# Dense q and k for layer 1, scattered into per-head strips by on-chip transfers

## Chip, core and metric

The kernel runs on one core of a Trainium2 chip. The core has a matrix engine (PE in the profile, with its weight loads as PEld), a vector engine (DVE), a scalar engine (ACT), GpSimd (POOL) and the sync engine (SP), which here only issues transfers. The metric is the device time of one execution in microseconds (us). The kernel before takes 1684.3 us, the median of three runs (1683.4 to 1684.37).

## What is computed

Sixteen sequences of 512 tokens with 128 channels pass through two layers. Layer 0 is linear attention followed by a mixture of eight experts with two chosen per token, plus a shared expert. Layer 1 is attention with sixteen heads of eight channels, in chunks of 64 queries, and a channel mix after it. The change touches only how the q and k of layer 1 are made. Cut to that:

```python
# layer 1 attention, for each chunk of 64 queries [s:e]
scores = einsum('bhtd,bhsd->bhts', q[:, :, s:e], k[:, :, :e]) / 8 ** 0.5   # 16 heads, d = 8
probs  = softmax(scores)                     # then a gate on the row sums
out    = einsum('bhts,bhsd->bhtd', probs, v[:, :, :e])
```

All data are float32.

## The kernel before, in words

The whole program is one stream of Python calls that are first recorded and then put in order. Every call on an engine becomes an `Op` with a cost, and `Program.run` (L330) is a list scheduler: for each engine it keeps the operations whose inputs are ready by its own reckoning, and emits the one recorded first (L407, with a preference for DVE operations that empty PSUM). The emitted order is fixed per engine, so on the chip each engine goes through its list in that order and stands still when the next one's input isn't there. The reckoning of a transfer is at L274: 80 ns on SP, and a size at 250 bytes per ns plus 2000 ns until it has landed (L379 to L385). PE's costs are at L261 to L271, with a charge for every change of the tile's shape (`TURN`, L220).

Four chains of work are recorded in turns: dispatch of tokens to experts, the expert tiles (`slot_tiles`, L1122), layer 0 (`first_layer`, L1499), and layer 1 (`layer1`, L1554). In layer 1 each sequence b has a `head` (L1510), which adds the experts' results, makes the layer norm `xp`, the channel mix, the values and the operands of the first half of the heads, and a `body` (L1529), which runs the two halves u = 0 and 1 of eight heads. `weighted(b, u)` (L1349) computes the scores again in transposed form (`st`), their exponentials (`ex`, ACT) and the output (`o`). Beside it runs the next thing: `operands(b, 1)` during `weighted(b, 0)`, with two of its steps for each of five units, and `head(b + 1)` during `weighted(b, 1)`, with three.

`operands` (L1294) is what is changed. There are 32 sets (b, u). A set holds eight heads as four strips of 32 partitions, two heads to a strip. In `qa` the rows 0 to 15 of a strip are the q of its two heads; the others carry a mask and, later, minus the row maximum. In `ka` there are two copies, one for each head of the pair; each copy has the other head's rows at zero, and rows that hold constant ones. To get this layout straight from the matmul, the weights `wqk1` are padded with zero columns (L584 to L588): 4 blocks of 128 columns for q and k of both halves. A set then needs these instructions:

```python
ps = big(f"qk1_{b}_{u}")
for i in range(2):                                   # q, k: 128x128 by 128x512
    M.matmul(ps[:, i, :], wqk1[:, 2 * i + u, :, :]..., xT, start=True, stop=True)
V.tensor_tensor(qa, ps[:, 0, :], c_("aug_q"), ALU.add)
for o in range(2):
    V.scalar_tensor_tensor(ka[:, o, :], ps[:, 1, :], c_("parity")[:, o : o + 1],
                           aug_k[:, o, :], ALU.mult, ALU.add)
```

After them come five units of score matmuls (`sc`) whose row maxima DVE takes (`maxima`), a transpose of the maxima (`mx`), and a subtraction in place, `qa -= pm` (L1345). `qa` and `ka` have two buffers each, so the `ka` of a set takes the place of the one two sets earlier, when the last `st` of that set is done. Before layer 1 starts, sequence 1 of layer 0 borrows the same buffers (`LENT`, L808).

SP issues every direct transfer: for each of 163 expert tiles a load of `wf` and one of `wp` (L1146, L1149; four buffers each), the token rows `xg`, the results `yg`, the passing of `xnT` and `x1` through DRAM, and the outputs.

Of the kernel before, what the change touches and what calls it, by code (L numbers as in the profile page):

```python
# [36 lines left out]
P = 128  # L37
# [15 lines left out]
def slot_count(gt):  # L53
# [29 lines left out]
_CONST = (  # L83
    ("ident", P), ("cos", NT * 4), ("sin", NT * 4), ("blocks", 8 * (PAIR + 2)), ("pick", 4),
    ("causal", P), ("rank", E), ("upper", P), ("ones", P), ("tile", SLOT_TILES),
    ("aug_q", T), ("aug_k", 2 * T), ("parity", 2),
)


# [68 lines left out]
class Base:  # L158


    def __init__(self, slots, make):
        self.slots, self.make, self.tile = slots, make, None
        self.writers, self.readers = [], []
        self.left, self.free_at, self.users = 0, 0.0, []

    def made(self):
# [58 lines left out]
class Program:  # L225
# [21 lines left out]
    def call(self, name, api, method, args, kw):  # L247
        views = [a for a in (*args, *kw.values()) if isinstance(a, View)]
        o = kw.get("out", args[0] if args else None)
        writes = [o.base] if isinstance(o, View) else []  # L250
        reads = [v.base for v in views if v is not o]
        n = math.prod(o.shape[1:]) if isinstance(o, View) else 0
        later = 0.0

        def made(a):
            return a.made() if isinstance(a, View) else a

        def emit():
            return getattr(api, method)(*map(made, args), **{k: made(a) for k, a in kw.items()})  # L259

        if name == "PE":  # L261
            later = 60.0
            form = (args[1].shape[0], o.shape[0])
            if method == "transpose":
                cost = 112.0
            elif args[1].shape[0] == 32:
                cost = max(0.425 * n, 56.0)
            elif o.shape[0] == 32:
                cost = max(0.425 * n, 56.0)
            else:  # L270
                cost = max(1.68 * n, 224.0)  # L271
        elif method == "dma_start":
            cost, later = 80.0, 512.0 * n
        else:  # L274
            form = method if (name, method) in COSTS else None
            if name == "DVE" and method in ("tensor_scalar", "tensor_scalar_min", "tensor_scalar_max"):
                form = "fast"
            if method in ("tensor_reduce", "bn_stats"):
                n = math.prod(args[1].shape[1:])
            least, each = COSTS[name, form]  # L280
            cost = least + each * n
            if kw.get("func", args[2] if len(args) > 2 else None) == AF.Sqrt:
                cost += 2600.0
        op = self.add(name, emit, reads, writes, cost, later)
        if name == "PE":
            (self.unit_of[0] if self.unit_of else op).form = form
        return op

    def add(self, name, emit, reads, writes, cost, later=0.0):
        if self.unit_of is not None:  # L290
            if self.unit_of == []:
                self.unit_of.append(self._new(name, None, 0.0, 0.0))
            op = self.unit_of[0]
            part = Op(name, emit, 0.0, 0.0, op.index)
            op.parts.append(part)
            op.cost += cost
        else:
            part = op = self._new(name, emit, cost, later)
        for base in reads:
            op.needs.update(base.writers)  # L300
        for base in writes:

            op.needs.update(o for o in base.writers if o.engine != "SP" or name != "SP")
            op.needs.update(base.readers)
        for base in reads:
            base.readers.append(op)
        for base in writes:
            if base.readers:
                base.writers, base.readers = [], []
            base.writers.append(op)  # L310
        op.needs.discard(op)
        op.bases.update(reads, writes)
        op.wrote.update(writes)
        return part
# [172 lines left out]
def two_layers(ctx: ExitStack, tc: tile.TileContext, x, small, const, w_fc, w_proj, out):  # L487
# [30 lines left out]
        i.behind = [(first, mybir.DependencyClass.NoSync)]  # L518


    const_sb = fixed.tile([P, _CONST_N], F32, tag="const", name="const_sb")
    small_sb = fixed.tile([P, _STAYS_N], F32, tag="small", name="small_sb")

    wfc_s = fixed.tile([P, FF], F32, tag="wfc_s", name="wfc_s")
# [10 lines left out]
        for n in ("xnT", "x1") for b in range(B) if n == "x1" or b > 1  # L535
    }
    x_in = {b: load_x(b, "x_in", 2) for b in range(2)}
    lo = _CONST_AT["aug_q"][0]
    SP.dma_start(const_sb[:, 0:lo], const[:, 0:lo])
    raw = {}  # L540
    for name in ("wqkv0", "wqk1"):
        program.lag = 400 if name == "wqk1" else 0
# [3 lines left out]
    for names in (_STAYS[:2], _STAYS[2:]):  # L546
# [1 line left out]
        (lo, _), (_, hi) = _SMALL_AT[names[0]], _SMALL_AT[names[-1]]  # L548
        (slo, _), (_, shi) = _STAYS_AT[names[0]], _STAYS_AT[names[-1]]
        SP.dma_start(small_sb[:, slo:shi], small[:, lo:hi])  # L550
    lo = _CONST_AT["aug_q"][0]
    SP.dma_start(const_sb[:, lo:], const[:, lo:])
    program.lag = 250
    SP.dma_start(wfc_s, w_fc[:, E, :])
    SP.dma_start(wpj_s, w_proj[:, E, :, :])
# [21 lines left out]
    rank = c_("rank").unsqueeze(1)  # L577
    cos = c_("cos").rearrange("p (t d) -> p t d", d=4)
    sin = c_("sin").rearrange("p (t d) -> p t d", d=4)
    aug_k = c_("aug_k").rearrange("p (o t) -> p o t", o=2)  # L580

    program.lag = 200

    wqk1 = fixed.tile([P, 4, 4, 32], F32, tag="wqk1", name="wqk1")  # L584
    G.memset(wqk1, 0.0)
    given1 = raw["wqk1"].rearrange("p (su j o e) -> p su j o e", su=4, j=4, o=2)
    for o in range(2):
        V.tensor_copy(wqk1[:, :, :, o * DH : (o + 1) * DH], given1[:, :, :, o, 0:DH])  # L588

    program.lag = 1000  # L590

# [699 lines left out]
            )  # L1291
        return vp

    def operands(xT, b, u):  # L1294

        ps = big(f"qk1_{b}_{u}")
        for i in range(2):
            M.matmul(
                ps[:, i, :], wqk1[:, 2 * i + u, :, :].rearrange("p j e -> p (j e)"), xT,
                start=True, stop=True,
            )
        qa = p2.tile([P, T], F32, tag="qa", name=f"qa_{b}_{u}")
        V.tensor_tensor(qa, ps[:, 0, :], c_("aug_q"), ALU.add)
        ka = p2.tile([P, 2, T], F32, tag="ka", name=f"ka_{b}_{u}")
        for o in range(2):  # L1310
            V.scalar_tensor_tensor(
                ka[:, o, :], ps[:, 1, :], c_("parity")[:, o : o + 1], aug_k[:, o, :],
                ALU.mult, ALU.add,
            )
        yield
        mx = maxima
        for i, unit in enumerate(QUERIES):
            scs = [big(f"sc1_{b}_{u}_{i}_{pr}") for pr in range(2)]
            with program.unit():
                for t, os_, at in unit:  # L1320
                    n, m = (t + 1) * P, len(os_)
                    for j in range(4):
                        r = 32 * j
                        M.matmul(
                            scs[j // 2][:, j % 2, at : at + m * n].rearrange(
                                "p (o k) -> p o k", o=m
                            ),
                            qa[r : r + 32, t * P : (t + 1) * P],
                            ka[r : r + 32, os_[0] : os_[0] + m, 0:n], start=True, stop=True,
                        )  # L1330
            for pr, sc in enumerate(scs):
                for t, os_, at in unit:
                    n, m = (t + 1) * P, len(os_)
                    V.tensor_reduce(
                        mx[:, t, 2 * pr : 2 * pr + 2, PAIR + os_[0] : PAIR + os_[0] + m],
                        sc[:, :, at : at + m * n].rearrange("p j (o k) -> p j o k", o=m), AX.X,
                        ALU.max,
                    )
            yield
        pm = one(f"mx1_{b}_{u}")  # L1340
        for t in range(NT):
            M.transpose(
                pm[:, t * P : (t + 1) * P], mx[:, t, :, :].rearrange("p j e -> p (j e)"), ident
            )
        V.tensor_tensor(qa, qa, pm, ALU.subtract)  # L1345
        yield
        return qa, ka

    def weighted(qm, ka, vp, b, u, ahead, n_ahead):  # L1349

# [159 lines left out]
    def head(b):  # L1510
# [8 lines left out]
        G.memset(xp[:, 0:1], 0.0)  # L1519
        yield from layernorm_T(x1, xp[:, 1 : T + 1], f"1_{b}", "xn1", 1)  # L1520
        yield
        base = yield from channel_mix(x1, xp, b)
        yield
        vp = values(xp[:, 1 : T + 1], b)
        yield
        qm, ka = yield from operands(xp[:, 1 : T + 1], b, 0)
        return xp, base, vp, qm, ka

    def body(b, state):  # L1529


        xp, base, vp, qm, ka = state
        o0, (qm, ka) = yield from weighted(
            qm, ka, vp, b, 0, operands(xp[:, 1 : T + 1], b, 1), 2
        )
# [64 lines left out]
def _constants():  # L1600
# [12 lines left out]
    c["blocks"] = (head == row[:, None, None]).astype(f).reshape(P, -1)  # L1613
    c["pick"] = ((i // DH) % 4 == np.arange(4)[:, None]).T.astype(f)
    aug_q, aug_k = np.zeros((4, 32, T), f), np.zeros((4, 32, 2, T), f)
    parity = np.zeros((4, 32, 2), f)
    for o in range(2):
        aug_k[:, PAIR + o, o] = 1.0
        parity[:, o * DH : (o + 1) * DH, o] = 1.0
    for t in range(NT):  # L1620
        aug_q[:, PAIR + 2 + t, t * P : t * P + P // 2] = HIDDEN
        aug_k[:, PAIR + 2 + t, :, t * P + P // 2 : (t + 1) * P] = 1.0
    c["aug_q"], c["aug_k"] = aug_q.reshape(P, T), aug_k.reshape(P, 2 * T)
    c["parity"] = parity.reshape(P, 2)
# [66 lines left out]
```

## Time and profile before

| | before |
|---|---|
| median of three runs | 1684.3 us |
| the profiled execution's own time | 1683.13 us |
| its span, first to last instruction | 1681.3 us |
| mean granted PE clock | 0.973 |
| PE busy | 1566.0 us (93%) |
| DVE busy | 1220.5 us (73%) |
| ACT busy | 763.4 us (45%) |
| POOL busy | 405.0 us (24%) |
| transfers of the SP queue | 148.67 MB, 29.7% of 16 engines |

The profile shows one execution. A group of instructions is named by the tile that it writes and those that it reads (`qk<-xp,wqk` writes the PSUM tile qk1 from xp and wqk1); L259 stands on almost every row, because one helper records every operation. One float32 matmul of the program stands as two PE records, so the 64 matmuls of `qk` are 128 records. PE records overlap, so the time that a group takes up on PE is read from the starts in the timeline, not from the sum of its durations.

### The profile page before, as it was taken

The numbers are of one execution on the slowest core, as the hardware profiler recorded it, in microseconds if no ns is written. First come the engines' busy times: TensorE is split into PE (matmuls) and PEld (weight loads), VectorE is DVE, ScalarE is ACT, GpSimd is POOL, SyncE is SP. The second block draws the span as 40 slices with busy tenths as digits, with TensorE's granted clock in tenths as the row PEclk, the third lists the DMA queues.
The fourth block names the chain that finished last, engine by engine and source line by source line (L and its number), as shares of the span: only waits on it lengthen the run. The fifth ranks groups of instructions, "written<-read, shape, count | busy, mean of one in ns | idle before, by whom it ended". The sixth has DMA issues, their size and how long they took to land.

```text
span 1681.3 us, 36447 instructions
## 1 busy us (share of the span) xinstructions
PE 1566.0 (93%) x14503; PEld 1027.3 (61%) x14503; DVE 1220.5 (73%) x2520; ACT 763.4 (45%) x1175; POOL 405.0 (24%) x389
## 2 busy tenths in 40 slices
PE   5898889999999999999999999999999999999996
PEld 3687766576756566665766656656665566555443
DVE  7876269767479875977678884968587867676773
ACT  3343334535445554445445553453545543534434
POOL 2404362162115211251014321140115010104000
PEclk8899999999999999999999999999999999999888
DMA  5377857143433532332332332313133223011000
GB/s 173 110 219 223 247 185 218 47 136 98 125 96 94 162 93 69 116 95 75 95 98 81 103 95 79 103 60 114 49 93 89 63 72 101 8 44 29 19 1 13
DMA packets 155129, 167.78 MB, mean 100 GB/s; under 512 B 13264, under 2 KB 100688, under 8 KB 154960
## 3 DMA queue, kind: packets, MB, share of 16 engines
q1 hardware_dynamic: 146768, 148.67, 29.7%
q0 software_dynamic: 8192, 16.79, 3.2%
q8 instruction: 114, 1.87, 0.4%
q14 instruction: 55, 0.45, 0.1%
HBM read 123.59 MB, written 41.81 MB: 98 GB/s over the span
## 4 chain that ended last, share of the span: by engine, by line
PE 55%; DVE 13%; ACT 3%; issue 1%; ACTq 0%; DVEq 0%
PE sc L259 11%; PE o L259 10%; PE st L259 8%; PE yg_ps L259 5%; DVE maxima L259 4%; PE hg_ps L259 4%; PE y L259 4%; PE qk L259 3%; PE h_ps L259 2%; ACT ex L259 1%; PE ho_a L259 1%; PE qkv L259 1%; PE oh_a L259 1%; PE mx L259 1%; PE cm_r L259 1%
## 5 line engine op out<-in xcount | busy, mean ns | idle before, releaser
L259 DVE TENSOR_REDUCE maxima<-sc 128x2 f32<-128x768 f32 (+2 forms) x448 | 385.4, 913 | 74.4 <-PE sc L259 71.4
L259 ACT ACTIVATE ex<-st 128x1024 f32<-128x1024 f32 x320 | 312.4, 1025 | 183.2 <-PE st L259 174.0
L259 PE MATMUL sc<-ka,qa 32*128 32x512 f32 (+2 forms) x1792 | 214.5, 518 | 7.5 <-DVE maxima L259 3.9
L259 PE MATMUL st<-qa,ka 32*128 32x384 f32 (+3 forms) x2048 | 209.3, 467 | 9.3 <-ACT ex L259 4.6
L259 DVE TENSOR_TENSOR am<-sc,const_sb 128x1024 f32<-128x1024 f32 x128 | 151.3, 1217 | 81.5 <-PE sc L259 76.6
L259 PE MATMUL yg_ps<-wp,hg 128*128 128x128 f32 x1304 | 182.1, 283 | 18.4 <-DVE hg L259 6.3
L259 PEld LDWEIGHTS yg_ps<-wp,hg 128*128 128x128 f32 x1304 | 160.0, 192 | 61.3 <-issue 32.1
L1091 POOL DMA_INDIRECT rows<-xn,pl_slot x128 | 131.4, 1026 | 224.0 <-DVE pl_slot L259 46.8
L259 PE MATMUL hg_ps<-xgT,wf 128*128 128x128 f32 x1304 | 176.1, 280 | 9.0 <-DMA wf<-in_w_fc 3.6
L1110 POOL DMA_INDIRECT back<-results,pl_slot x128 | 127.2, 994 | 220.2 <-PE st L259 45.6
L259 PEld LDWEIGHTS hg_ps<-xgT,wf 128*128 128x128 f32 x1304 | 158.7, 193 | 32.9 <-issue 13.4
L259 PE MATMUL o<-ex,vpad 128*32 128x512 f32 (+3 forms) x2048 | 175.7, 445 | 1.1 <-ACT oT_a L259 0.6
L259 PEld LDWEIGHTS st<-qa,ka 32*128 32x128 f32 x2048 | 103.6, 185 | 78.1 <-issue 27.0
L259 ACT ACTIVATE hg<-hg_ps 128x1024 f32<-128x1024 f32 x84 | 84.0, 1000 | 137.0 <-PE hg_ps L259 123.0
L259 PEld LDWEIGHTS sc<-ka,qa 32*128 32x128 f32 x1792 | 90.5, 188 | 69.0 <-issue 21.4
L259 POOL TENSOR_TENSOR hg<-hg 128x1024 f32<-128x1024 f32 x34 | 65.1, 1914 | 276.4 <-ACT hg L259 276.1
L259 PEld LDWEIGHTS o<-ex,vpad 128*32 128x32 f32 x2048 | 52.5, 109 | 88.0 <-issue 66.0
L259 DVE TENSOR_TENSOR hg<-hg 128x1024 f32<-128x1024 f32 (+1 forms) x50 | 58.4, 1168 | 59.3 <-ACT hg L259 45.7
L259 ACT COPY oTs<-o 128x256 f32<-128x256 f32 (+1 forms) x96 | 42.6, 444 | 125.4 <-PE o L259 113.6
L259 PE MATMUL sc<-q0m,k0T 32*128 32x256 f32 x1024 | 82.1, 412 | 3.3 <-ACT ex L259 1.4
L259 ACT COPY yg<-yg_ps 128x256 f32<-128x256 f32 x84 | 31.0, 369 | 112.5 <-PE yg_ps L259 77.0
L259 PE MATMUL o<-am,vpad 128*32 128x128 f32 x2048 | 77.0, 277 | 1.2 <-DVE am L259 0.9
(189 smaller groups left out, 2216.8 us busy)
## 6 DMA issues: line engine op xcount, KB each, us to landing
wf<-in_w_fc SPq DMA_DIRECT2D x163, 256.0 KB
wp<-in_w_proj SPq DMA_DIRECT2D x163, 256.0 KB
results<-yg SPq DMA_DIRECT2D x79, 128.0 KB
xg<-rows SPq DMA_DIRECT2D x37, 256.0 KB
rows<-zeros SPq DMA_DIRECT2D x2, 2496.0 KB
x_in<-in_x SPq DMA_DIRECT2D x16, 256.0 KB
x<-x SPq DMA_DIRECT2D x16, 256.0 KB
out<-rr SPq DMA_DIRECT2D x16, 256.0 KB
```

The source lines that it names most:

```text
L259: return getattr(api, method)(*map(made, args), **{k: made(a) for k, a in kw.items()})
L1091: i = nc.gpsimd.indirect_dma_start(out=rows.made()[:, :], out_offset=bass.IndirectOffsetOnAxis(ap=slot.made(), axis=0), in_=row.made(), in ...
L1110: "POOL", lambda: nc.gpsimd.indirect_dma_start(out=o.made(), out_offset=None, in_=results.made()[:, :], in_offset=bass.IndirectOffsetOnAxi ...
```

## The change

Per sequence, q and k of all sixteen heads are made by two matmuls from packed weights (`dense`), and two ACT copies put them into SBUF as `q1` and `k1`; this stands in `head`, after the layer norm and before the channel mix. `q1` uses the buffer of the layer norm's `xn`. The strips are now two lasting pairs of buffers, one for each half, filled once from the constants; in each set twelve transfers by SP overwrite only the rows of q and k: four of 16 rows and eight of 8 rows, each row 512 floats. The zero rows and the ones stay as they are. The subtraction of the maxima writes a tile of its own, `qm`. The three DVE operations of a set, the tile `parity`, the memset of the padded weights and the load of the masks at the start are gone. In the scheduler, writes that follow each other to one buffer all wait for the readers from before the first of them, and the landing time of a transfer now counts the partitions of its destination.

```diff
-            cost, later = 80.0, 512.0 * n
+            cost, later = 80.0, 4.0 * n * (o.shape[0] if isinstance(o, View) else P)
...
             op.needs.update(base.readers)
+            op.needs.update(base.before)
...
             if base.readers:
+                base.before = base.writers + base.readers
                 base.writers, base.readers = [], []
...
-    wqk1 = fixed.tile([P, 4, 4, 32], F32, tag="wqk1", name="wqk1")
-    G.memset(wqk1, 0.0)
...
+    wqk1 = fixed.tile([P, 2, P], F32, tag="wqk1", name="wqk1")
+    given1 = raw["wqk1"].rearrange("p (h e) -> p h e", e=32)
+    V.tensor_copy(
+        wqk1.rearrange("p s (h e) -> p (s h) e", e=DH), given1[:, :, 0:DH]
+    )
...
+    def make_strips():
+        for u in range(2):
+            qa = p2.tile([P, T], F32, tag="qa", name=f"qa_{u}")
+            ka = p2.tile([P, 2, T], F32, tag="ka", name=f"ka_{u}")
+            (lo, hi), (klo, khi) = _CONST_AT["aug_q"], _CONST_AT["aug_k"]
+            first = [
+                SP.dma_start(qa, const[:, lo:hi]),
+                SP.dma_start(ka.rearrange("p o t -> p (o t)"), const[:, klo:khi]),
+            ]
+            strips.append((qa, ka, first))
+
+    def dense(xT, b):
+
+        if not strips:
+            make_strips()
+        ps = big(f"qk1_{b}")
         for i in range(2):
...
+            M.matmul(ps[:, i, :], wqk1[:, i, :], xT, start=True, stop=True)
+        q = p2.tile([P, T], F32, tag="xn1", name=f"q1_{b}", bufs=1)
+        k = p2.tile([P, T], F32, tag="k1", name=f"k1_{b}", bufs=1)
+        S.copy(q, ps[:, 0, :])
+        S.copy(k, ps[:, 1, :])
+        return q, k
+
+    def operands(qk, b, u):
+
+
+        q, k = qk
+        qa, ka, first = strips[u]
+        for j in range(4):
+            at, r = u * P // 2 + j * PAIR, 32 * j
+            rows = [SP.dma_start(qa[r : r + PAIR, :], q[at : at + PAIR, :])]
+            for o in range(2):
+                rows.append(SP.dma_start(
+                    ka[r + o * DH : r + (o + 1) * DH, o, :], k[at + o * DH : at + (o + 1) * DH, :]
+                ))
+            for i in rows if first else ():
+                after(i, first)
+        strips[u] = (qa, ka, [])
         yield
...
-        V.tensor_tensor(qa, qa, pm, ALU.subtract)
-        yield
-        return qa, ka
+        qm = p2.tile([P, T], F32, tag="qm", name=f"qm_{b}_{u}")
+        V.tensor_tensor(qm, qa, pm, ALU.subtract)
+        yield
+        return qm, ka
...
+        qk = dense(xp[:, 1 : T + 1], b)
+        yield
         base = yield from channel_mix(x1, xp, b)
         yield
         vp = values(xp[:, 1 : T + 1], b)
         yield
-        qm, ka = yield from operands(xp[:, 1 : T + 1], b, 0)
-        return xp, base, vp, qm, ka
+        qm, ka = yield from operands(qk, b, 0)
+        return qk, base, vp, qm, ka
```

More of the change, by code (lines that the diff above doesn't have):

```diff
@@ L85 @@
     ("causal", P), ("rank", E), ("upper", P), ("ones", P), ("tile", SLOT_TILES),
-    ("aug_q", T), ("aug_k", 2 * T), ("parity", 2),
+    ("aug_q", T), ("aug_k", 2 * T),
 )
@@ L162, in __init__ @@
         self.slots, self.make, self.tile = slots, make, None
-        self.writers, self.readers = [], []
+        self.writers, self.readers, self.before = [], [], []
         self.left, self.free_at, self.users = 0, 0.0, []
@@ L518, in follows @@
         i.behind = [(first, mybir.DependencyClass.NoSync)]
-    const_sb = fixed.tile([P, _CONST_N], F32, tag="const", name="const_sb")
+    const_sb = fixed.tile([P, _CONST_AT["aug_q"][0]], F32, tag="const", name="const_sb")
     small_sb = fixed.tile([P, _STAYS_N], F32, tag="small", name="small_sb")
@@ L537, in two_layers @@
     x_in = {b: load_x(b, "x_in", 2) for b in range(2)}
-    lo = _CONST_AT["aug_q"][0]
-    SP.dma_start(const_sb[:, 0:lo], const[:, 0:lo])
+    SP.dma_start(const_sb, const[:, 0 : _CONST_AT["aug_q"][0]])
     raw = {}
@@ L550, in two_layers @@
         SP.dma_start(small_sb[:, slo:shi], small[:, lo:hi])
-    lo = _CONST_AT["aug_q"][0]
-    SP.dma_start(const_sb[:, lo:], const[:, lo:])
     program.lag = 250
@@ L579, in two_layers @@
     sin = c_("sin").rearrange("p (t d) -> p t d", d=4)
-    aug_k = c_("aug_k").rearrange("p (o t) -> p o t", o=2)
     program.lag = 200
-    wqk1 = fixed.tile([P, 4, 4, 32], F32, tag="wqk1", name="wqk1")
-    G.memset(wqk1, 0.0)
-    given1 = raw["wqk1"].rearrange("p (su j o e) -> p su j o e", su=4, j=4, o=2)
-    for o in range(2):
-        V.tensor_copy(wqk1[:, :, :, o * DH : (o + 1) * DH], given1[:, :, :, o, 0:DH])
+    wqk1 = fixed.tile([P, 2, P], F32, tag="wqk1", name="wqk1")
[3 more added lines that the diff above has]
+    )
     program.lag = 1000
@@ L1292, in values @@
         return vp
-    def operands(xT, b, u):
-        ps = big(f"qk1_{b}_{u}")
-        for i in range(2):
[L1303 to L1314, printed above, removed]
+    strips = []
+    def make_strips():
[12 more added lines that the diff above has]
+        ps = big(f"qk1_{b}")
+        for i in range(2):
+            M.matmul(ps[:, i, :], wqk1[:, i, :], xT, start=True, stop=True)
[17 more added lines that the diff above has]
+        strips[u] = (qa, ka, [])
         yield
@@ L1525, in head @@
         yield
-        qm, ka = yield from operands(xp[:, 1 : T + 1], b, 0)
-        return xp, base, vp, qm, ka
+        qm, ka = yield from operands(qk, b, 0)
+        return qk, base, vp, qm, ka
     def body(b, state):
-        xp, base, vp, qm, ka = state
+        qk, base, vp, qm, ka = state
         o0, (qm, ka) = yield from weighted(
-            qm, ka, vp, b, 0, operands(xp[:, 1 : T + 1], b, 1), 2
+            qm, ka, vp, b, 0, operands(qk, b, 1), 2
         )
@@ L1615, in _constants @@
     aug_q, aug_k = np.zeros((4, 32, T), f), np.zeros((4, 32, 2, T), f)
-    parity = np.zeros((4, 32, 2), f)
     for o in range(2):
         aug_k[:, PAIR + o, o] = 1.0
-        parity[:, o * DH : (o + 1) * DH, o] = 1.0
     for t in range(NT):
@@ L1623, in _constants @@
     c["aug_q"], c["aug_k"] = aug_q.reshape(P, T), aug_k.reshape(P, 2 * T)
-    c["parity"] = parity.reshape(P, 2)
     inv = (f(10000.0) ** (-np.arange(4, dtype=f) / f(4))).astype(f)
```

## The prediction, made before the changed kernel had run

> **What bounds the kernel now.** I read the page first, then busy time by stage, then the timelines around the operation that is changed. The page says who is full:
>
> ```profile
> PE 1566.0 (93%) x14503; PEld 1027.3 (61%) x14503; DVE 1220.5 (73%) x2520; ACT 763.4 (45%) x1175; POOL 405.0 (24%) x389
> ```
>
> An average over stages can mislead, so busy time by stage (columns: length, then PE, PEld, DVE, ACT, POOL with their counts, clock, DMA share, GB/s):
>
> ```profile
> 330.00:700.00 370.00, 357.00 (x3400) 239.24 (x3399) 273.69 (x538) 176.75 (x277) 105.21 (x95) 0.99 0.37 111
> 700.00:1100.00 400.00, 388.66 (x3669) 250.87 (x3668) 307.18 (x635) 192.71 (x289) 100.57 (x91) 0.99 0.31 92
> 1100.00:1500.00 400.00, 386.41 (x3647) 241.96 (x3646) 296.74 (x532) 189.39 (x284) 71.87 (x67) 1.00 0.24 71
> 1500.00:1600.00 100.00, 93.33 (x846) 49.83 (x843) 70.60 (x140) 46.15 (x60) 21.14 (x20) 0.95 0.08 23
> 1600.00:1681.00 81.00, 63.74 (x509) 30.89 (x507) 45.45 (x96) 29.68 (x41) 2.92 (x3) 0.82 0.03 7
> ```
>
> From 330 to 1500 us PE is busy 1132.07 of 1170 us, 97%: what leaves PE there comes off the time almost whole. After 1600 PE is busy 79%, and latencies count. Next, what the changed operation takes on PE, and what surrounds it (timeline of PE, sequence 6):
>
> ```profile
> 843.28 1.02 PE L259 MATMUL qk<-xp,wqk 128*128 128x512 f32 x2
> 844.23 1.13 PE L259 MATMUL cm_v<-small_sb,xk 128*128 128x128 f32 x8
> 845.19 1.02 PE L259 MATMUL qk<-xp,wqk 128*128 128x512 f32 x2
> ...
> 848.71 1.14 PE L259 MATMUL sc<-ka,qa 32*128 32x512 f32 x8
> ...
> 874.87 1.88 PE L259 MATMUL qk<-xp,wqk 128*128 128x512 f32 x4
> 876.59 0.60 PE L259 MATMUL mx<-const_sb,maxima 128*128 128x128 f32 x4
> ```
>
> Two qk matmuls (four records) hold PE from 874.87 to 876.59, 1.72 us, so one is 0.86 us. They stand in a gapless row. DVE's part is in the groups by shape:
>
> ```profile
> L259 DVE SCALAR_TENSOR_TENSOR ka<-qk,const_sb 128x512 f32<-128x512 f32 x64 | 45.6, 742 | 0.0
> L259 DVE TENSOR_TENSOR qa<-qk,const_sb 128x512 f32<-128x512 f32 x32 | 22.0, 689 | 21.6 <-PE qk L259 21.4
> ```
>
> And SP, which gets the new work; its timeline at the start, where it issues without waiting, and the row of its waits for a transfer:
>
> ```profile
> 3.29 0.43 SPq L259 DMA_DIRECT2D wfc_s<-in_w_fc  x1
> 3.77 0.43 SPq L259 DMA_DIRECT2D wpj_s<-in_w_proj  x1
> 4.24 0.43 SPq L259 DMA_DIRECT2D raw_wqk<-in_small  x1
> ```
> ```profile
> SPq L259 <- DMA x<-xs: 15.1, 8, 3.5
> ```
>
> One issue every 0.47 us. The second row is a load that waits for a 256 KB store: 15.1 / 8 = 1.9 us, with the issue (0.33 us) about 2.2 us from issue to landing.
>
> **Part by part.** *PE, removed.* 64 matmuls become 32: 32 x 0.86 = 27.5 us. Two of sixteen sequences (14, 15) have theirs after 1500 us, where PE is not quite full; I still count all.
>
> *DVE, removed.* 45.6 + 22.0 = 67.6 us of DVE's 1220.5. DVE is second; what PE waits for it in the list of PE's waits is a few microseconds here and there (4.2 for sc, 3.8 for st, 3.0 for hg_ps, 2.5 for mx, all on maxima: 13.5 us). About a third of that should go: 4 us. Bounds: 0 (the waits on maxima are a latency and not a queue) and 13.5.
>
> *ACT, added.* 32 copies of 128x512 from PSUM; the nearest row is oT_a<-oh_a, 587 ns: 18.8 us on an engine that is 45% busy. Hidden, unless an exponential (1025 ns) queues behind: 1.2 us per sequence, 19 us in all if nothing covered it. They also give the PSUM tile back sooner than the three DVE operations did, which need 2.1 us. I take 0.
>
> *SP, added: the disputed step.* 12 x 32 = 384 issues x 0.47 = 180 us of SP. Each burst lasts 12 x 0.47 = 5.6 us, and its last transfer lands some 2.2 us later by the row above: 7.8 us. The bytes (128 rows of 2 KB per set, 8.4 MB beside 148.67) don't matter. Behind each burst wait the loads of wf and wp, the results and xg. The weights have four buffers and PE waited only 3.6 us in all for wf, with over 20 us between two pairs of tiles' hg_ps in the timeline around 800 to 900 us, so 5.6 us of delay is covered; without that cover every burst would cost up to 5.6 us. The scheduler books 80 ns for an issue, so it thinks a burst over in 1 us and may place sc up to 12 x 0.39 = 4.7 us early. So I compare the latency with the room that the old order had. For u = 1 the transfers may go once the last st of the set two earlier is done; q1 and k1 are there long before. From that st to the first sc, read off the PE timeline for the 16 sets, the room is 12.5 to 33.6 us (sequence 11 has the 12.5). Needed: 7.8, or about 10 with two weight loads ahead. No stall. For u = 0 the chain starts at the copy xp on ACT: dense 1.72, two copies 1.2, transfers 7.8, in all 10.7 us. The room from the end of xp (or of the last st, if later) to the first sc is 13.2 to 15.8 us in eight sequences, 22 to 32 in five, and 9.3, 5.9 and 9.2 us in sequences 0, 14 and 15. Some 1 us in each of the eight, where an exponential or a weight load gets in between, plus 1.4 + 4.8 + 1.5 in the three: about 16 us. Bounds: 8 (only the three) and 32 x 4.7 = 150 (every sc stands for what SP was underestimated); I stay near the lower one, because the room is measured.
>
> [...] If each paid its 2.2 us in turn, a burst would be 26 us, over nearly all the room above: some 15 us for each u = 0 set and 10 for each u = 1, +400 us. The SP rows show issues 0.47 us apart while a landing takes 2 us, so the overhead overlaps and only the issue adds up. I take the row.
>
> *PE, added waits.* Each sc must now see transfers landed, twelve semaphores per set in place of DVE's one. [...] some become separate instructions in PE's queue. The page does not count those; in the records of the trace PE has 332 semaphore instructions with a median of 51 ns. Bounds: 0, and 384 x 51 ns = 20 us. With three extra for a set: 32 x 3 x 0.05 = 5 us.
>
> *Moved or small.* The mask load of 769 KB leaves the start and 1.5 MB of strip filling comes before sequence 0's sc; no PE row waits there for masks: -1 us at most, +2 if the filling is late; I take 0. `qm` in place of the subtraction in place is the same DVE work. `q1` in the buffer of xn makes the next layer norm wait for the u = 1 transfers; those go out at the start of `weighted(b, 0)`, the next norm is worked on mostly during `weighted(b, 1)`: 0.
>
> Sum: -27.5 - 4 + 16 + 5 = -10.5 us. Against the profiled execution (1681.3 span, 1683.13 whole) that is 1672.6; the median of the runs is 1.2 above that execution, so 1673.8 on its scale. I forecast 1674.
>
> **The rivals.** *Arrivals set the pace (slower).* The place is the first sc of the u = 0 sets, after a chain of engine handovers that the scheduler books 4 to 5 us too short. Each time, PE stands still, as its order can't be changed. The saved part, without stalls, is 27.5 + 4 - 5 = 26.5 us; from 26.5 / 32 = 0.8 us per set on, or 1.7 us per u = 0 set, this decides. Against it: the room of 13 us and more in thirteen of sixteen. For it: the new order is not the old one; the scheduler fills PE by its own reckoning and may draw sc forward into that room, and DVE is no longer there to hold it back. With 2.7 us on all u = 0 sets: 16 x 2.7 = 43, 1684.3 - 26.5 + 43 = 1701.
>
> *All of PE's saving and more.* If the room holds everywhere but at the three, and DVE's relief is worth its 13.5 us: -27.5 - 13.5 + 8 + 3 = -30, so 1654. For it: DVE is 75% busy from 330 to 1500 us (877.61 of 1170), and the maxima gate sc.
>
> *No difference.* The new order simply has other gaps: stalls of 26 us eat what was saved: 1684. For it, PE is idle 38 us from 330 to 1500, for dozens of small reasons, any of which a new order can double.
>
> That the change doesn't do what it says is out: the transfers cover rows 0 to 15 of a strip and the constants are below, and matmuls are halved by construction.
>
> **How the numbers follow.** Likeliest case (most of the saving kept, 1665 to 1680): 0.40. Full gain (below 1665): 0.20. No difference: 0.10. Slower by arrivals: 0.30. Measurements of this kernel tell 0.2%, or 3.4 us, from no change. So faster 0.60, same 0.10, slower 0.30. The range from 1652 to 1704 leaves out about 0.05 below and 0.15 above.
>
> **What would show it.** In the changed profile, qk should hold 64 records in place of 128, PE busy should be some 25 to 30 us less, DVE about 65 less, ACT about 19 more. Right about the stalls: PE's waits on qa and ka transfers (sc and its weight loads released by DMA) add up to 10 to 20 us, most of it in sequences 0, 14 and 15. Wrong: over 30 us of them spread over all u = 0 sets, or PE waits for wf or xg grown to several times 3.6 us, or a last stage (from 1500) longer by more than 10 us.

## The result, and the profile after

The changed kernel takes 1748.32 us, the median of four runs (1741.22 to 1755.99), beside 1684.34 us for the kernel before on the same chip (1683.4 to 1687.69): a ratio of 1.0383 with a 95% interval of 1.0344 to 1.0422. It is 64 us slower; the forecast was 1674, with a range up to 1704. The profiled execution took 1750.56 us with a span of 1748.8 us.

The page of the changed kernel, its row of busy times and the row of the granted clock:

```profile
PE 1595.2 (91%) x14439; PEld 1039.3 (59%) x14439; DVE 1155.9 (66%) x2423; ACT 780.9 (45%) x1209; POOL 407.6 (23%) x388
...
PEclk8899999999999999999999899989999999999988
```

The work changed as forecast: PE has 64 records fewer, DVE is busy 65 us less, ACT 18 more. Yet PE is busy 29 us *longer* with less to do, and the mean granted clock fell from 0.973 to 0.952. Busy time by stage (length, PE, PEld, DVE, ACT, POOL with their counts, clock, DMA share, GB/s) shows where:

```profile
330.00:700.00 370.00, 339.84 (x3244) 229.27 (x3244) 242.88 (x481) 175.17 (x272) 104.08 (x94) 0.97 0.37 109
700.00:1100.00 400.00, 372.19 (x3386) 238.38 (x3385) 263.08 (x526) 183.94 (x277) 93.08 (x84) 0.96 0.32 92
1100.00:1500.00 400.00, 381.90 (x3582) 239.03 (x3580) 288.81 (x567) 189.76 (x289) 78.19 (x70) 0.98 0.28 82
```

From 330 to 1500 us PE was busy 97% before; now it is 1093.93 of 1170, 93.5%, at clocks of 0.96 to 0.98 where they were 0.99 and 1.00. So PE stands still more often in the middle, and runs slower there too. What it stands for is in PE's waits (us in total, times, longest); first the row of the kernel before, then three of the changed one:

```profile
PE hg_ps L259 <- DMA wf<-in_w_fc: 3.6, 3, 1.8
```
```profile
PE hg_ps L260 <- DMA wf<-in_w_fc: 30.0, 13, 8.6
PE ln_ps L260 <- DVE xn L260: 21.2, 5, 10.0
...
PE sc L260 <- DMA ka<-k: 8.1, 10, 1.9
```

`hg_ps`, the first matmuls of an expert tile, waited 3.6 us for its weights `wf` before; now 30.0. The wait of `sc` for the strips, which the prediction worked on most, is 8.1 us. The late transfers are mainly not the new ones but the weight loads *behind* them. SP's timeline at the largest case (start, us, instruction):

```profile
443.23 0.38 SPq L260 DMA_DIRECT2D xg<-rows  x1
456.12 5.00 SPq L260 DMA_DIRECT2D qa<-q  x8
461.22 5.43 SPq L260 DMA_DIRECT2D ka<-k  x8
467.98 0.37 SPq L1145 DMA_DIRECT2D wf<-in_w_fc  x1
```

and PE's over the same time:

```profile
461.20 1.15 PE L260 MATMUL sc<-q0m,k0T 32*128 32x256 f32 x16
470.91 2.04 PE L260 MATMUL hg_ps<-xgT,wf 128*128 128x128 f32 x8 [8.57 <-DMA wf<-in_w_fc]
```

Sixteen transfers go out in one row: the twelve of u = 0 and the four `qa` of u = 1, which are ready as soon as `q1` exists. They hold SP from 456.12 to 466.65 us, 10.5 us. Only then come the loads of the next tile. `wf` is issued at 467.98, and PE, whose order is fixed, stands 8.57 us until 470.91. The eight matmuls behind it take 2.04 us. In the kernel before, sixteen of the same form took 2.05 us, so these eight ran at half the speed. Busy time by stage in short windows around it:

```profile
452.00:462.00 10.00, 10.00 (x120) 6.58 (x116) 5.52 (x9) 5.65 (x9) 1.57 (x1) 1.00 0.11 27
462.00:471.00 9.00, 0.43 (x9) 0.12 (x1) 2.35 (x2) 0.00 (x0) 0.00 (x0) 0.79 0.26 74
471.00:478.00 7.00, 7.00 (x50) 4.67 (x50) 0.43 (x1) 2.09 (x3) 1.04 (x1) 0.79 0.45 131
```

The clock is 1.00 before the stall. In the trace's clock records it is at half from 467.15 us, when PE has stood 4.8 us, to 473.97; PE is busy in the last 3.1 of these 6.8 us, and half of that, some 1.5 us, is lost (an estimate from the eight matmuls that took the time of sixteen). So the stall is paid once standing, 8.6 us, and a smaller second time slow. Most of the half-clock stretches have no such stall before them. The changed kernel has 26, of 3.4, 6.8 or 10.2 us (the last is 13.9). In the 10 us before seven of them PE stands in a gap that is 4.9 to 10.0 us long as a whole; before the other 19 the longest gap is 0.5 to 2.3 us. That the long gaps bring on the seven is an inference from their order; what starts the other 19, no run here shows. Within the span the stretches add up to 90 us before and 169 us after.

That gives an account of the whole span, 67.5 us longer in the two profiled executions; it is worked out by laying the clock records over PE's records. PE's idle time (span less busy) went from 115.3 to 153.6 us, +38.3; the waits for `wf` are 26.4 of it and those of `sc` for the strips 8.1. Of PE's busy time 65.8 us were at half clock before and 135.6 after; half of it is lost by the same estimate, which is 34.9 us more. The three longest waits for `wf` (20.4 us) are followed by only 10.4 us of slow work; most of the rest comes after the short gaps. With slow time counted half, PE's work is 1533.1 us before and 1527.4 after, only 5.7 less: `qk` lost 28.7, but `sc` gained 11.3 and other groups the rest. The sum closes: 38.3 + 34.9 - 5.7 = 67.5.

### The profile page after: what moved, and what is told of

Read it like the earlier page. It is cut to its first block, busy times and chain, and to the rows that moved or that the text cites. A ratio compares the mean times of both kernels' runs of the same rounds, so it can differ in the third digit from the quotient of the medians.

```text
span 1748.8 us, 37035 instructions
## 1 busy us (share of the span) xinstructions
PE 1595.2 (91%) x14439; PEld 1039.3 (59%) x14439; DVE 1155.9 (66%) x2423; ACT 780.9 (45%) x1209; POOL 407.6 (23%) x388
## 4 chain that ended last, share of the span: by engine, by line
PE 68%; DVE 13%; ACT 7%; issue 5%; SPq 4%; DMA 3%; POOL 0%; ACTq 0%; DVEq 0%; POOLq 0%
PE sc L260 13%; PE o L260 12%; PE st L260 8%; PE yg_ps L260 8%; PE hg_ps L260 6%; PE y L260 5%; DVE maxima L260 4%; SPq L260 3%; PE h_ps L260 3%; DMA wf<-in_w_fc 2%; PE qkv L260 2%; ACT ex L260 2%; PE qk L260 2%; PE ho_a L260 1%; PE cm_v L260 1%
## 5 line engine op out<-in xcount | busy, mean ns | idle before, releaser
L260 PE MATMUL sc<-ka,qa 32*128 32x512 f32 (+2 forms) x1792 | 235.3, 530 | 15.8 <-DMA ka<-k 8.1
L260 PE MATMUL st<-qm,ka 32*128 32x384 f32 (+3 forms) x2048 | 209.2, 470 | 8.2 <-DVE maxima L260 5.8
L260 PE MATMUL hg_ps<-xgT,wf 128*128 128x128 f32 x1304 | 183.0, 285 | 34.1 <-DMA wf<-in_w_fc 30.0
L260 PE MATMUL yg_ps<-wp,hg 128*128 128x128 f32 x1304 | 186.8, 288 | 19.2 <-DVE hg L260 9.3
L260 PE MATMUL o<-ex,vpad 128*32 128x512 f32 (+3 forms) x2048 | 179.9, 456 | 0.5 <-ACT ex L260 0.3
L260 PEld LDWEIGHTS sc<-ka,qa 32*128 32x128 f32 x1792 | 96.2, 192 | 90.9 <-issue 34.3
L260 PEld LDWEIGHTS st<-qm,ka 32*128 32x128 f32 x2048 | 104.1, 188 | 76.9 <-issue 26.5
L260 POOL TENSOR_TENSOR hg<-hg 128x1024 f32<-128x1024 f32 x34 | 65.8, 1934 | 348.5 <-ACT hg L260 337.4
L260 DVE TENSOR_TENSOR hg<-hg 128x1024 f32<-128x1024 f32 (+1 forms) x50 | 58.5, 1170 | 63.7 <-ACT hg L260 63.5
L260 PE MATMUL sc<-q0m,k0T 32*128 32x256 f32 x1024 | 87.2, 420 | 8.4 <-ACT ex L260 3.4
```

## Experiments

Four theories were written down first. **A**: the slow issues of the strips hold up SP's queue, the weights come late, PE stands and its clock drops. **B**: `sc` waits for the strips themselves. **C**: the next layer norm waits for the buffer that `q1` shares with `xn`. **D**: the scheduler's new order is worse by chance. Medians stand beside the kernel before on the same chip; brackets are 95% intervals of the ratio.

**1. The change without its transfers.** Everything else stays: one dense pair of matmuls, the copies, the lasting strips.

```diff
         qa, ka, first = strips[u]
-        for j in range(4):
-            at, r = u * P // 2 + j * PAIR, 32 * j
-            rows = [SP.dma_start(qa[r : r + PAIR, :], q[at : at + PAIR, :])]
...
-            for i in rows if first else ():
-                after(i, first)
```

> The changed kernel without the twelve transfers of each set: the strips keep only the constants they are filled with once, so the scores are computed from zeros and the output is not the reference's. Dense matmuls, copies, qm and all else stay. Theory A (the transfers hold up SP's queue, the weight loads wf behind them come late, PE stands and falls to half its clock): 1650 to 1668 us, PE's wait for wf back at 4 us, half-clock time back near 90 us. Theory B (scores stand for the strips' arrival) and theory C (the next layer norm waits for q1's buffer, and DVE with it): the same, since both waits go with the transfers. Theory D (the new order of the scheduler is worse by chance, whatever the transfers cost): stays above 1700 us.

1654.76 against 1687.84 us, 0.9809 [0.9788, 0.9830]. Its page:

```profile
PE 1541.4 (93%) x14439; PEld 1018.6 (62%) x14439; DVE 1158.9 (70%) x2423; ACT 779.8 (47%) x1209; POOL 407.8 (25%) x388
```

PE has the same 14439 records as the changed kernel and is busy 53.8 us less; the clock is 0.975 and the wait for `wf` is 0.4 us. So the rest of the change is worth -33 us, a little more than the -26.5 that the prediction gave it (-27.5 - 4 + 5), and with the transfers it is some 95 us slower (1748 against 1655). That speaks against D, but doesn't settle it: with no transfers to place, the scheduler made another order (at 3973 of the 14439 places of PE's list another instruction stands). B and C lose their transfers here as well, so they stay.

**2. A buffer of its own for `q1`** (two pairs of small routing tiles share their buffers to make room, which the diff below leaves out).

```diff
-        q = p2.tile([P, T], F32, tag="xn1", name=f"q1_{b}", bufs=1)
+        q = p2.tile([P, T], F32, tag="q1", name=f"q1_{b}", bufs=1)
```

> The changed kernel with q1 in a buffer of its own and not in that of the layer norm's xn (two pairs of small routing tiles share their buffers to make room). Theory C: DVE's waits of xn for the transfers of q (38 us in the changed kernel) go, and 25 to 40 us of the time with them: 1710 to 1723 us. Theory A: the wf waits stay at about 30 us, and the time falls by at most 10 us: 1738 to 1748 us.

1744.87 against 1687.84, 1.0325 [1.0298, 1.0351]. In the changed kernel DVE's waits have these rows:

```profile
DVE xn L260 <- DMA qa<-q: 22.5, 5, 9.1
...
DVE xn L260 <- DMA ka<-k: 15.6, 2, 8.9
```

Here both are gone, and the time is hardly less: the two intervals overlap. PE's wait for `wf` is 33.1 us. PE's order is nearly that of the changed kernel (8 of its 14439 places differ), so the 38 us that DVE no longer waits had cost little or nothing. C isn't the main cause.

**3. The scheduler is told what such a transfer costs SP**: 660 ns in place of 80, for transfers to 8 or 16 rows. The program's operations stay the same, only their order changes.

```diff
-            cost, later = 80.0, 4.0 * n * (o.shape[0] if isinstance(o, View) else P)
+            few = isinstance(o, View) and o.shape[0] in (8, 16)
+            cost, later = 660.0 if few else 80.0, 4.0 * n * (o.shape[0] if isinstance(o, View) else P)
```

> The changed kernel with the scheduler told that a transfer of 8 or 16 rows costs SP 660 ns (the spacing in the changed kernel's trace) and not 80 ns; only the order that it makes can change. Theory A: the weight loads are placed before or between the transfers, PE's wait for wf falls from 30 us to under 10, and the time to 1690 to 1715 us. Theory B: sc is placed later and its 8 us of waits go, 1735 to 1742. Theory C: DVE's wait of xn is the same or longer, 1740 to 1750.

1699.83 against 1687.84, 1.0065 [1.0043, 1.0086]. The row of PE's waits:

```profile
PE hg_ps L260 <- DMA wf<-in_w_fc: 7.9, 8, 3.0
```

The same 384 transfers cost about 50 us less once the order expects them. Half-clock time falls from 169 to 137 us. This speaks for A and for the 80 ns as part of the cause, but an order that is new is also a test of D, so A needs a proof that leaves the changed kernel aside.

**4 and 5. The same transfers beside the kernel before, read by nobody.** In every set of the *old* kernel, rows of `xp` are written to a spare tile that nothing uses: twelve transfers of 16 and 8 rows (512 bytes a row), or one transfer of 128 rows. The diffs leave out the spare tile itself and the two pairs of routing tiles that share their buffers for it.

```diff
+        for j in range(4):
+            at, r = u * P // 2 + j * PAIR, 32 * j
+            SP.dma_start(spare[r : r + PAIR, 0:P], xT[at : at + PAIR, 0:P])
+            for o in range(2):
+                SP.dma_start(
+                    spare[r + o * DH : r + (o + 1) * DH, P:], xT[at + o * DH : at + (o + 1) * DH, 0:P]
+                )
```
```diff
+        SP.dma_start(spare[:, 0:P], xT[:, 0:P])
```

> The kernel before, with twelve transfers per set added beside it: the same row counts and issue places, from xp to a spare tile that nobody reads, rows of 512 bytes (two pairs of small routing tiles share their buffers to make room). Nothing waits for these transfers but SP's own queue. Theory A: slower than before by 30 to 70 us, 1715 to 1755 us, with PE waiting 15 to 40 us for wf. Theories B and C: 1684 to 1690 us, since no score and no layer norm waits for them. Theory D: within 10 us of before.

> The kernel before with one transfer per set beside it, of 128 rows of 512 bytes from xp to a spare tile: the same bytes and the same place as the twelve beside the kernel before, in one issue. If the number of issues on SP is what costs (theory A): within 5 us of before, PE's waits for wf under 8 us. If it is the bytes, or a transfer at this place in SP's order as such (SP stands for xp with the weight loads behind it): 1705 to 1745 us.

Twelve: 1747.66 against 1687.84, 1.0363 [1.0338, 1.0388]. One: 1684.56 against 1684.97, 0.9994 [0.9978, 1.0009]. Of the twelve, the row of PE's waits and the spare tile's own row (shortest, median and longest issue in ns, first and last start):

```profile
PE hg_ps L259 <- DMA wf<-in_w_fc: 30.5, 11, 7.7
```
```profile
L259 SPq DMA_DIRECT2D spare<-xp x384: 535/624/1565, 245.3 to 1674.1; - x192
```

Of the one:

```profile
L259 SPq DMA_DIRECT2D spare<-xp x32: 465/471/549, 241.5 to 1601.7; - x32
```

The stall of the changed kernel is there again with the twelve; a line of SP's timeline and one of PE's:

```profile
456.90 15.57 SPq L259 DMA_DIRECT2D spare<-xp  x24
```
```profile
476.56 1.65 PE L259 MATMUL hg_ps<-xgT,wf 128*128 128x128 f32 x6 [7.73 <-DMA wf<-in_w_fc]
```

This shows that the issues alone are enough. No instruction reads the spare tile, so B and C can't act, and nothing of the change is there. (That `xp` has one more reader is common to both experiments.) D can't be the cause of most of it: PE, DVE and ACT keep the order of the kernel before, record for record, up to 1034.6 us, and at that place the kernel is already 45 of its 63 us behind. Its span is accounted for: PE stands 41.4 us more (26.9 of it for `wf`; 11.3 in one wait for ACT, which waited for an output transfer issued behind a burst) and loses 21.9 us more to half clock, while its work at full clock is within 1 us of before. One transfer in place of twelve, with the same 64 KB, costs nothing that can be measured; the order stays that of before (4 of PE's 14503 places differ). What costs is the number of issues.

The size is not that of the changed kernel. These transfers cost 60 us and come in longer bursts, those of the change cost some 95. What lies between is not shown by itself; the changed kernel also has the 8.1 us for which `sc` waits for the strips, and `sc`'s slower matmuls (below).

**6. Four transfers of 16 rows per set beside the kernel before**, the first line of that loop only: is the cost in proportion?

> The kernel before with only the four 16-row transfers per set beside it (128 issues in place of 384; 536 ns each in the run with twelve). Theory A in its simple form, loss in proportion to the issues: a third of the 60 us that twelve cost, so 1700 to 1710 us. Theory A with a cover: a weight load is issued some microseconds before PE needs it, so a burst of four or eight (2 to 5 us) is covered more often than one of 12 to 24: 1684 to 1695 us, PE's wait for wf under 10 us.

1680.51 against 1677.1, 1.0018 [1.0006, 1.0031], with these rows:

```profile
PE hg_ps L259 <- DMA wf<-in_w_fc: 4.1, 4, 1.6
```
```profile
L259 SPq DMA_DIRECT2D spare<-xp x128: 507/549/1484, 243.8 to 1600.7; - x128
```

A third of the issues costs 3 us (1 to 5 by the interval), all of them 60. Two sets' transfers mostly go out together: of the 18 bursts here, 14 hold eight transfers and last 5 to 6 us, and with the twelve 14 of 18 hold 24 and last about 16 us. The short ones are mostly covered by the lead that a weight load has (its distribution stands further below), the long ones are not. So the cost is not a price per transfer.

**7. Booked as in 3, and `q1` in its own buffer as in 2.**

> Booked at 660 ns, and q1 in a buffer of its own. With the booking alone DVE's xn still waited 13 us for the transfers of q. If that wait costs time once the wf waits are gone (theory C as the second term): 1680 to 1693 us. If it is covered: 1695 to 1705, as booked.

1688.38 against 1684.97, 1.0011 [0.9988, 1.0033]. The difference between 3 and 7 is 0.0054, 9 us. In 3, DVE's `xn` still waited 13.1 us for `qa`; here it waits for no strip. So C is the likely second term, once `wf` is no longer in front of it; the order of the two kernels differs too.

**8 and 9. Other issuing engines**, booked: ACT, and GpSimd (booked at 1000 ns; the indirect transfers that it issues in the kernel before take 994 and 1026 ns on average).

```diff
-            rows = [SP.dma_start(qa[r : r + PAIR, :], q[at : at + PAIR, :])]
+            rows = [S.dma_start(qa[r : r + PAIR, :], q[at : at + PAIR, :])]
...
-                rows.append(SP.dma_start(
+                rows.append(S.dma_start(
```

> Booked at 660 ns, with the transfers issued by ACT and not by SP. Theory A: SP is as it was before, PE's wait for wf is at 4 us or below, but ACT gets some 240 us of issues (45% to about 60% busy) and the exponentials queue behind bursts: between 1665 and 1700 us, below the booked SP version by 5 to 30 us. If the transfers cost by their landing and not by their queue: about 1700, as on SP.

> The transfers issued by GpSimd, booked at 1000 ns. Theory A: SP is free, and GpSimd has room (23% busy, 384 issues of about 1 us make it 45%): 1660 to 1690 us, unless the gathers and scatters that share its queue come late, which would show as waits on back or rows.

ACT: 1710.78 against 1684.97, 1.0137 [1.0102, 1.0172]. GpSimd: 1694.04, 1.0049 [1.0029, 1.0068]. Both miss what was expected, ACT clearly. With ACT, SP's waits have a row that the booked version on SP doesn't have:

```profile
SPq L260 <- DMA ka<-k: 152.5, 12, 47.4
```

SP's loads now wait for transfers that ACT issued. In the trace of the changed kernel SP's 960 transfers take turns on eight semaphores, 120 on each, and 932 of them wait for the one on which their own landing is counted. With ACT issuing, the trace has the transfers of both queues in turn on the same eight, and at each of these 12 waits the transfer that SP issues next counts on the very semaphore that it waited for. So the two queues were not independent. With GpSimd issuing, the trace has about 510 ns for each issue, and GpSimd's busy time goes from 408 to 599 us; the wait for `wf` falls to 3.8 us, and still the interval overlaps that of 3.

**10. Fewer issues: by way of DRAM.** `q1` and `k1` are written once per sequence, in three transfers, to an image of the strips in DRAM whose constant rows are already there; each set reads its two strips with two transfers of 128 rows. That is 7 issues per sequence in place of 24. `q1` has its own buffer, and the weights' columns are put so that `k1` comes in the order of the image.

```diff
+        SP.dma_start(qd[:, 0:PAIR, :], q)
+        for o in range(2):
+            SP.dma_start(kd[:, 17 * o : 17 * o + PAIR : 2, :], k[64 * o : 64 * o + 64, :])
...
-        for j in range(4):
...
+        SP.dma_start(qa, qd[4 * u : 4 * u + 4, :, :].rearrange("s r t -> (s r) t"))
+        SP.dma_start(
+            ka.rearrange("p o t -> p (o t)"),
+            kd[4 * u : 4 * u + 4, :, :].rearrange("s (r o) t -> (s r) (o t)", o=2),
+        )
```

> Dense q and k as in the change, but put into strips by way of DRAM: per sequence three transfers write q1 and k1 into a DRAM image of the strips whose constant rows were filled once, and per set two transfers of 128 rows read the image back. Seven issues per sequence in place of 24, more bytes (about 2 MB per sequence in place of 0.5), one more landing in the chain; q1 in its own buffer, few-row transfers booked at 660 ns. If what is left between the booked version with its own buffer (1686) and no transfers at all (1655) is SP's issue time: 1655 to 1668 us. If it is the latency of strips that come by transfer, or their landing: 1685 to 1700, as the chain is now longer.

1681.07 against 1684.66, 0.9974 [0.9962, 0.9986]: the fastest whole version, 0.26% below the kernel before. It lies in neither of the expected ranges. Had the issues been all that was left, it would have come within some 10 us of experiment 1; about 28 us are missing (0.9974 - 0.9809 = 0.0165). In the profiled executions its span is 30.3 us above that of experiment 1: PE's idle time is 6.4 more (115.2 against 108.8) and busy time 23.9 (1565.3 against 1541.4). Of its busy time 100.7 us are at half clock against 60.5, which is some 20 of the 23.9. Its waits for `wf` are only 4.8 us, so this slow time doesn't come from them; what it comes from is not shown.

**11 and 12. Every transfer booked at its cost, and a control.** Experiment 10 with 430 ns for every ordinary transfer, 620 for one of few rows, and 1750 in place of 300 for a tile's pair of weight loads (from one pair of `wf` and `wp` to the next it is 1.74 us behind the stall above, from 467.98 to 469.72); and the kernel *before* with 430 and 1750, whose diff this is.

```diff
-            cost, later = 80.0, 512.0 * n
+            cost, later = 430.0, 512.0 * n
...
-            program.add("SP", emit, [expert.base], [wf.base, wp.base], 300.0, 4.0 * P * 2 * FF)
+            program.add("SP", emit, [expert.base], [wf.base, wp.base], 1750.0, 4.0 * P * 2 * FF)
```

> As the version through DRAM, with every SP operation booked near what the trace shows: 430 ns a transfer, 620 ns one of few rows, 1750 ns the pair of weight loads with its register load. If SP's true cost in the scheduler's reckoning still matters with few issues: 5 to 10 us below the version through DRAM; otherwise within 5 us of it.

> The kernel before with the same booking of SP (430 ns a transfer, 1750 ns a pair of weight loads), as the control: its SP has no bursts and PE waits only 3.6 us for wf, so within 6 us of before. If it falls by more, part of a gain of the booked versions is not the change's.

1690.45 against 1684.66, 1.0033 [1.0016, 1.0049], and for the control 1701.77, 1.0091 [1.0068, 1.0115]. Both were missed: the first is 9 us slower than experiment 10, where none or a gain was expected, and the control, expected within 6 us, loses 17. Its operations are those of before, only in another order (PE's list differs at more than half of its places; ACT has two table loads more). So truer costs don't always give a better order, and an order alone was worth 1% here. How much of the 28 us between experiments 10 and 1 is the order, and how much the longer way of q and k, stays open. The same holds for a part of the 50 us that booking won in experiment 3; experiments 4 to 6 don't hang on it, as their order is that of before, with the twelve for the first 1035 us.

## Why the prediction was wrong

**PE, DVE and ACT, removed and added work: right.** `qk` has 64 records in place of 128, and DVE and ACT moved by what was said. PE's busy time was to fall by 25 to 30 us and rose by 29, for the reasons below. Experiment 1, the change without the transfers, measured -33 us against -26.5.

**Stalls of `sc` on the strips: inside their bounds, and too high.** 16 us were forecast with bounds of 8 and 150, 8.1 were measured. All that care went into a step that was not the one to fail, and the rival "arrivals set the pace" has the right sign at the wrong place: the late arrival is mainly that of `wf` at `hg_ps`.

**PE, added waits: the number right, the cost probably too low.** 96 more semaphore instructions were forecast in PE's queue; there are 423 against 332 before and 325 in experiment 1. The forecast gave them 5 us. At full clock `sc` takes 207 us of PE in the changed kernel, 196 before and 193 in experiment 1, and 200 to 208 in every version that scatters rows into the strips against 192 to 197 in the others. That these instructions are the reason is not shown.

**"SP, added: the disputed step": here it failed. The burst was sized too short, and the cover that was to hide it was not there; a term for the clock was missing as well.**

*The issue.* 0.47 us was taken from loads of 128 rows. The new transfers' own rows, with the filling of the strips from `const` (128 rows) for comparison:

```profile
L260 SPq DMA_DIRECT2D ka<-k x256: 624/625/1278, 254.7 to 1679.6; - x128
```
```profile
L260 SPq DMA_DIRECT2D qa<-q x128: 507/582/1658, 249.5 to 1668.0; - x128
```
```profile
L260 SPq DMA_DIRECT2D ka<-in_const x2: 323/325/327, 86.8 to 87.6; - x2
```

Eight rows take SP 625 ns, sixteen 582. With the gaps between, one comes every 0.63 to 0.68 us in the stall above. The bursts mostly don't hold twelve either: u = 1's `qa` are often ready with u = 0's transfers. Counted without another transfer or a pause of 1 us between, nine bursts hold sixteen transfers and last 10.5 us or more, three hold 24 and last 16 to 18, fourteen hold eight and last mostly 5.7, and eight are of other sizes. The prediction had 5.6 us for all. The 384 issues take 243 us in place of 180, and SP is issuing 472 us in all, where it was 240.

*The cover.* "The weights have four buffers … with over 20 us between two pairs of tiles' hg_ps … so 5.6 us of delay is covered." The reading of the timeline is wrong even for that window. Two rows of it, with no other `hg_ps` between them:

```profile
896.66 1.95 PE L259 MATMUL hg_ps<-xgT,wf 128*128 128x128 f32 x16
900.84 2.05 PE L259 MATMUL hg_ps<-xgT,wf 128*128 128x128 f32 x16
```

They start 4 us apart, and the other groups of `hg_ps` there 1 to 26. And four buffers say how early a load *may* go out, not how early it *does*. Measured in the kernel before, from the issue of a tile's `wf` to its first `hg_ps`, the lead of the 163 tiles has a median of 11.0 us; a quarter have less than 7.0, a tenth less than 5.5, the least 2.9; nearly half have less than 10.5. An example from the kernel before, one line of SP's timeline and one of PE's:

```profile
1041.26 0.34 SPq L1146 DMA_DIRECT2D wf<-in_w_fc  x1
```
```profile
1044.67 2.05 PE L259 MATMUL hg_ps<-xgT,wf 128*128 128x128 f32 x16
```

The sixteen matmuls belong to two tiles; this `wf` is the second tile's, whose eight start at 1045.66, 4.4 us after the issue. Of that lead the landing takes about 3 us (467.98 to 470.91 in the stall above). A burst of 10.5 us uses up leads like these. What was put at nothing came to 30.0 us of waits for `wf` in place of 3.6. The prediction wrote down the price of a missing cover, "up to 5.6 us" a burst, and then didn't look for the smallest lead. 32 x 5.6 = 179 us was the bound on that side, and nothing of it came into the sum.

*The clock.* The sum had no term for half clock, and 34.9 us more were lost to it than before. Only some 5 us of that come right behind the three longest waits for `wf`; why the rest came with the change is not shown.

**"`q1` in the buffer of xn … 0": wrong.** DVE waited 38.1 us for these transfers (22.5 + 15.6). It cost little while PE stood for `wf` anyway (experiment 2), and perhaps up to 9 us once that was mended (3 and 7, whose orders differ).

**The landings paid in turn: rightly set aside, and the cost was beside them.** The +400 us, 2.2 us in turn for each transfer, were set aside because the overhead "overlaps and only the issue adds up". The first half was true: 128 small transfers cost 3 us in experiment 6, and the +400 us never came. But the issue that adds up *was* the cost, and the row that was taken for its duration showed issues of another shape.

The prediction had named its own test: "PE waits for wf or xg grown to several times 3.6 us". They are 8.3 times that.

## What to carry to other kernels

Reckon with an issuing queue as with an engine: multiply the new issues by the measured duration of an issue *of that shape* (here 384 took 243 us), and see what stands behind the burst and with how little lead it was issued before, in the smallest tenth (here under 5.5 us) and not in the mean. A number of buffers is not a lead: there were four here, and the least lead was 2.9 us. The cheapest proof of such a cause is to put the suspected transfers beside the old kernel, into a tile that nobody reads, and to look in the trace whether the order stayed the same. Where the granted clock falls, lay the slow stretches over the engine's busy time before pricing them: slow time in which it stands costs nothing more (in the changed kernel PE was busy in 135.6 of 169 us at half clock).

## What the runs showed of the hardware that was not expected

Of the transfers within SBUF, those of fewer rows took SP longer to issue. The medians are 471 ns for 128 rows of 512 bytes (experiment 5), 549 for 16 such rows (experiment 6), and in the changed kernel, with rows of 2 KB, 582 for 16 rows and 625 for 8, though each of these three moves fewer bytes than the first. From DRAM, 128 rows took 325 ns in the filling of `ka`. What takes the time is not shown.

Issuing from ACT didn't free SP's queue: SP waited 152.5 us in 12 waits for ACT's transfers, with which it shared eight semaphores.

The clock's share of this change was nearly as large as that of standing still: 38 us more idle, 35 us more lost to half clock. And most stretches at half clock began without a long stall: 19 of the 26 in the changed kernel had no gap of PE above 2.3 us in the 10 us before.
